# One reduction and one product for a group's counts, and a score leaky that reads PSUM, in a graph attention layer

## The chip, the core and the metric

The kernel runs on one core of a Trainium2 chip. The metric is the time of one execution on the device in microseconds; three runs of the kernel before give a median of 5057.35 us (5054.29 to 5057.92). The core's engines are called PE (matrix products; PEld is its weight load), DVE, ACT, POOL and SP as in the profile. Each runs its own instructions in order, and waits for the others by semaphores. SP only issues DMAs; POOL issues the indirect ones.

## The reference

A graph layer with 12500 nodes of 128 features and 412500 edges of 64 features, with 8 attention heads. The padded tables have 98 blocks of nodes. What matters of it:

```
h, q, k, v = x@Wn+bn, x@Wq+bq, x@Wk+bk, x@Wv+bv;   eh = edges@We + be
hmid   = leaky_relu(concat(q[src], k[tgt], eh) @ A1 + b1, 0.2)
scores = leaky_relu(hmid @ A2 + b2, 0.2)
w      = softmax(scores.mean(-1), over all edges)
out    = segment_sum(w[:, None] * v[tgt], src)
y      = layernorm(h + out) * gamma + beta;   result = layernorm(x + y)
```

The edges come sorted by target. The kernel needs them by source, since the sum runs over sources.

## The kernel before, in words

**Placing.** The edges are cut into 403 groups of 8 tiles of 128 edges, in six parts. For every group the kernel makes a record per edge (edge and target terms of the hidden layer, the value row, the source's lane) and writes the records to a table in DRAM that is ordered by block of source nodes. Where a record goes is counted on the chip: `oh` (L796) is a one-hot of each edge's block out of 99 (98 and a spare one), for 8 tiles as 2 halves of 4. `four` (L806) adds the halves, `few` (L808) adds the remaining four columns to two. PE's `count` (L816) sums `few` over the edges into `pc` in PSUM, one product for each of the two columns, once with the matrix `above` (edges ahead in the tile's lanes) before a group is placed and once with `rest` after it. `ats` (L834) and `pos` (L845) pick each edge's position from `pc`, `idx` (L847) makes it an index. `ohd` (L810) is the one-hot of the targets, by which PE fetches the target rows from `kvs` (L865), adds the edge terms (L871), and ACT copies the result to a record buffer `rec` (L882, L883; six buffers of four tiles). POOL sends each tile of records by an indirect DMA, here called a scatter (L894): 8 for a group, 3224 in all.

**Summing.** A unit is up to two blocks of source nodes with 10, 12 or 14 tiles of records. There are 294 units, 49 in each part. A unit's rows are loaded from the table (`rt`, L1028); its sources' lanes are masked (`sl`, L1050), turned on PE (L1058) into a PSUM tile of the pool `psc`, copied (`slT`, L1065), and spread over the lanes by two DMAs (L1072, L1077). One-hots of them (`ohT`, L1086) fetch the source terms into the hidden layer `ph` (L1097, L1106), whose leaky is a slope copy on ACT (`hm`, L1117) and a max on DVE (L1121). The scores come by L1134 into a PSUM tile of the same pool `psc`, which has **one buffer**: the turn of a later unit and the scores of this one share it. `biased` (L1149, ACT) adds `b2` on the way from PSUM to the SBUF tile `z`. `leaky_scores` (L1157, DVE) takes max(0.2 z, z) in place. `heads` (L1167) adds the heads on PE. Where the tiles of a unit do not divide by four, `biased` and `leaky_scores` have two pieces (96 lanes and 32), and so does each unit of 14 or 10 tiles: 245 units. `maxima`, `reference` and `weights` make the softmax's weights; `select` (`ohs`, L1215), `weigh` (`ohw`, L1229) and `add` (L1258) sum the weighted values.

**Order.** It is written out by hand. Each unit has a list of steps, 8 or 6 per unit. Of a unit that starts at step s with 14 tiles, the scores are at s+9, the bias at s+11, the leaky at s+12, the heads at s+14; the turn of the unit three later is at s+13. A part's units are summed while the next part is placed: a generator `make` yields six times a group, and the steps are dealt out evenly between its yields. What is left after the last group, the last part's 49 units, and the closing (two layer norms) runs without placing.

Of the kernel before, what the change touches and what calls it, by code (L numbers as in the profile page):

```python
# [10 lines left out]
FP = mybir.dt.float32  # L11
BF = mybir.dt.bfloat16
I32 = mybir.dt.int32
U8 = mybir.dt.uint8
AF = mybir.ActivationFunctionType
ALU = mybir.AluOpType
AX = mybir.AxisListType
# [3 lines left out]
P = 128  # L21
# [4 lines left out]
SLOPE = 0.2  # L26
NB = 7
GT = 8
# [334 lines left out]
def first_layer(nc, prep, pprep, WqT, WkT, WeT, Wv, Wn, A1, bq, bk, be, bv, bn, b1):  # L363

    A1s = prep.tile([D, 3, D], FP)
    nc.sync.dma_start(out=A1s, in_=A1.rearrange("(s k) d -> k s d", k=D))
    wT = prep.tile([D, 2, D], FP)
    nc.sync.dma_start(out=wT[:, 0, :], in_=WqT)
    nc.sync.dma_start(out=wT[:, 1, :], in_=WkT)
    weT2 = prep.tile([D, 2, DE], FP)  # L370
    for h in range(2):
        nc.sync.dma_start(out=weT2[:, h, :], in_=WeT)
    cols = prep.tile([D, 3], FP)
    for i, b in enumerate((bq, bk, be)):
        nc.sync.dma_start(out=cols[:, i : i + 1], in_=b)
    W = prep.tile([D, 4, D], FP)
    nc.sync.dma_start(out=W[:, 2, :], in_=Wv)
    nc.sync.dma_start(out=W[:, 3, :], in_=Wn)
    bias = prep.tile([P, 4, D], FP)
    nc.vector.memset(bias[:, 1, :], 0.0)  # L380
    nc.sync.dma_start(out=bias[:, 2, :], in_=bv.to_broadcast([P, D]))
    nc.sync.dma_start(out=bias[:, 3, :], in_=bn.to_broadcast([P, D]))
    b1_b = prep.tile([P, D], FP)
    nc.sync.dma_start(out=b1_b, in_=b1.to_broadcast([P, D]))

    pw = pprep.tile([P, 2, D], FP)
    for s in range(2):
        nc.tensor.matmul(pw[:, s, :], wT[:, s, :], A1s[:, s, :], start=True, stop=True)
    nc.vector.tensor_copy(W[:, 0:2, :], pw)
    pe = pprep.tile([P, D], FP)  # L390
    nc.tensor.matmul(
        pe, weT2.rearrange("k h f -> k (h f)"), A1s[:, 2, :], start=True, stop=True
    )
    WeS = prep.tile([P, D], FP)
    nc.vector.tensor_copy(WeS, pe)

    pb = pprep.tile([P, D], FP)
    for s in range(3):
        nc.tensor.matmul(
            pb, cols[:, s : s + 1].to_broadcast([D, P]), A1s[:, s, :],  # L400
            start=(s == 0), stop=(s == 2),
        )
    nc.vector.tensor_add(bias[:, 0, :], pb, b1_b)
    return W, WeS, bias
# [48 lines left out]
def sorted_path(  # L453
# [8 lines left out]
    nc = tc.nc  # L462
# [3 lines left out]
    NBK = nb + 1  # L466
    EG = GT * P

    const = ctx.enter_context(tc.tile_pool(name="const", bufs=1))
# [24 lines left out]
    nc.vector.memset(A2s, 0.0)  # L494
    nc.scalar.dma_start(out=A2s[:, :H], in_=A2)
    b2_c = const.tile([P, 1], FP)
    nc.vector.memset(b2_c, 0.0)
    headsum = const.tile([P, 4], FP)
    nc.vector.memset(headsum, 0.0)
    for j in range(4):  # L500
        nc.scalar.dma_start(out=b2_c[32 * j : 32 * j + H, :], in_=b2)
        nc.vector.memset(headsum[32 * j : 32 * j + 32, j : j + 1], 1.0)


    fmax = max(
# [12 lines left out]
    def fill(k, n):  # L518

        b, top = 0, plan.tiles[k]  # L520
        while b < nb:
            m = 1
            while m < n and b + m < nb and plan.fill[k][b + m] == plan.fill[k][b]:
                m += 1
            a = plan.cap // P - plan.fill[k][b]
            if a < top:
                yield b, m, a, top - a
            b += m

    def fill_top(k, n):  # L530

        top, most = plan.tiles[k], plan.cap // P
        if top < most:
            for b in range(0, nb, n):
                yield b, min(n, nb - b), top, most - top
# [43 lines left out]
    with tc.tile_pool(name="prep", bufs=1) as prep, tc.tile_pool(  # L579
        name="pprep", bufs=1, space=PSUM  # L580
    ) as pprep, tc.tile_pool(name="pnode", bufs=4, space=PSUM) as pnode:
        W, We_, bias = first_layer(
            nc, prep, pprep, WqT, WkT, WeT, Wv, Wn, A1, bq, bk, be, bv, bn, b1
        )
# [26 lines left out]
    start = const.tile([1, G], I32)  # L611
# [108 lines left out]
    lp = pool("plc", 2)  # L720
# [21 lines left out]
    data, ohds, ohs, few, ats, idxs = {}, {}, {}, {}, {}, {}  # L742
    firsts = []
    pcs = {}
# [15 lines left out]
    def make(p):  # L760


        g0, g1 = plan.parts[p]
# [28 lines left out]
        def onehots(g):  # L792
            if g >= G:
                return
            oh = lp.tile([P, 2, NBK, 4], BF)
            nc.vector.tensor_tensor(  # L796
                oh,
                blk[:, g * GT : (g + 1) * GT]
                .rearrange("p (h o t) -> p h o t", h=2, o=1).to_broadcast([P, 2, NBK, 4]),
                iotaE[:, :NBK, :].rearrange("p (o b) t -> p o b t", o=1)  # L800
                .to_broadcast([P, 2, NBK, 4]),
                op=ALU.is_equal,
            )

            four = one.tile([P, NBK, 4], BF, name="four")
            nc.vector.tensor_add(four, oh[:, 0, :, :], oh[:, 1, :, :])  # L806
            few[g] = lp.tile([P, NBK, 2], BF, name="few")
            nc.vector.tensor_add(few[g], four[:, :, :2], four[:, :, 2:])  # L808
            ohd = wp.tile([P, EG], BF)
            nc.vector.tensor_scalar(ohd, data[g][1], node, None, op0=ALU.is_equal)  # L810
            ohds[g], ohs[g] = ohd, oh


        def count(g, m):
            for i in range(GT // 4):
                nc.tensor.matmul(  # L816
                    pcs[p + (g >= g1)], m, few[g][:, :, i], start=False, stop=False, skip_group_check=True
                )

        def before(g):  # L820
            if g >= G:
                return
            if g == g1:
                ended()
                begin(p + 1)
            elif p == 0 and g == plan.gate:
                gated()
            count(g, above)
# [109 lines left out]
        if p == 0:  # L938
            firsts.append(const.tile([NP, NBK], FP, name="firsts"))
            nc.sync.dma_start(out=firsts[0], in_=bounds[:, 0, :])  # L940
            for g in range(4):
                load(g)
            onehots(0)
            begin(0)
            before(0)
            masked(0)
            places(0)
        for g in range(g0, g1):
            yield
            load(g + 4)  # L950
            if g == g0 + 2:
                limits()
            pk = rows(g, 0)
            after(g)
            onehots(g + 1)
            yield
            evacuate(g, 0, pk)
            yield
            before(g + 1)
            yield  # L960
            pk = rows(g, 2)
            masked(g + 1)
            yield
            evacuate(g, 2, pk)
            idxs.pop(g)
            places(g + 1)
            data.pop(g)
            ohds.pop(g)
            yield
# [19 lines left out]
    state = {}  # L989

    def sums_of(bp):
# [151 lines left out]
        def biased(i):  # L1143
            st = state[i]
            psc, pieces = st["z"]
            z = zp_.tile([P, 4 * P], FP, name="z")
            st["z"] = z, pieces
            for p0, p1, n in pieces:
                nc.scalar.activation(  # L1149
                    z[p0:p1, : n * P], psc[p0:p1, : n * P], AF.Identity, bias=b2_c[p0:p1, :]  # L1150
                )

        def leaky_scores(i):
            z, pieces = state[i]["z"]
            for p0, p1, n in pieces:
                zs = z[p0:p1, : n * P]
                nc.vector.scalar_tensor_tensor(zs, zs, SLOPE, zs, op0=ALU.mult, op1=ALU.max)  # L1157

        def heads(i, t0, m):
            st = state[i]  # L1160
# [124 lines left out]
        for i, (nt, nk, s0, load_at, f, e, turn_at) in enumerate(plans):  # L1285
# [7 lines left out]
            for k in range(nk):  # L1293
                c = 4 * k
                n, s = min(4, nt - c), s0 + 2 * k
# [4 lines left out]
            z = s0 + 2 * nk + 1  # L1300
            do(z, scores, i, 0, nt)
            do(z + 1 + e, biased, i)
            do(z + 2 + e, leaky_scores, i)
            do(z + 3 + 2 * e, heads, i, 0, nt)
            do(f, maxima, i)
# [5 lines left out]
            for j, t0 in enumerate(range(0, nt, 4)):  # L1311
                n = min(4, nt - t0)
# [265 lines left out]
    with tc.manual_schedule():  # L1578
        done = 0
        for p in range(NP + 1):  # L1580
# [8 lines left out]
            if p == 0:  # L1589
                i0 = 0  # L1590
                for k, i1 in enumerate((6 * plan.gate - 12, n0)):
                    pieces = list(fill(k, 2))
# [5 lines left out]
            if 0 < p <= TABS:  # L1598
                pieces = list(fill_top(p - 1, 2))
# [34 lines left out]
def kernel(tc, n, n_edges, x, xT, src, dst, dst_g, bounds, xN, *rest):  # L1634
    nc = tc.nc
    plan = Plan(n, n_edges, x.shape[1], src.shape[1] // GT)
    with tc.tile_pool(name="flag", bufs=1) as fpool:
        flag = fpool.tile([1, 1], I32)
        with ExitStack() as ctx:
            sorted_path(ctx, tc, plan, flag, x, xT, src, dst, dst_g, bounds, xN, *rest)  # L1640
        other = nc.values_load(flag[0:1, 0:1], min_val=0, max_val=1)
        with tc.If(other > 0):
            with ExitStack() as ctx:
                general(ctx, tc, n_edges, x, xT, src, dst, *rest)
# [60 lines left out]
```

## Time and profile before

| | |
|---|---|
| three runs, us | 5054.29, 5057.92, 5057.35 |
| the profiled execution, us | 5054.13 |
| its span, us | 5052.4 |
| mean granted TensorE clock | 0.904 |
| matmuls, DVE and ACT instructions in the page | 32676, 10011, 8487 |
| scatters (L894) | 3224 |

The profile is one execution. A row of groups gives line, engine, operation, tiles written and read with their shapes and count, then busy microseconds and the mean of one in ns, then the engine's idle time just before and who ended it. The rows of waits give engine, waiting line, who ended the wait, microseconds in total, times and the longest. A row of the timeline gives start and duration in microseconds; where it merges several instructions, xN says so and the duration is from the first one's start to the last one's end.

### The profile page before, as it was taken

How to read it: one execution, taken by the hardware profiler on the slowest of the kernel's cores; microseconds unless marked ns; L12 is line 12 of the kernel's file. 1: busy time of each engine (PE TensorE's matmuls, PEld its weight loads, DVE VectorE, ACT ScalarE, POOL GpSimd, SP SyncE). 2: the span in 40 equal slices, each digit the busy share in tenths (PEclk: the TensorE clock that was granted, in tenths of full speed). 3: DMA queues.
4: the chain of work that ended last, by engine and by line, in shares of the span. 5: the costliest groups of instructions: out<-in, count | busy, mean ns of one | idle time of the engine just before them, and what ended most of it. 6: DMA issues, size and time to landing. Idle time of an engine off the chain costs nothing.

```text
span 5052.4 us, 98033 instructions
## 1 busy us (share of the span) xinstructions
PE 4182.9 (83%) x32676; PEld 3101.9 (61%) x32676; DVE 4003.6 (79%) x10011; ACT 3266.3 (65%) x8487; POOL 3352.2 (66%) x3265
## 2 busy tenths in 40 slices
PE   3565568889888888899999899999899999899980
PEld 2343345666666666667776676776677776667760
DVE  6787666778777777789888788888789888777778
ACT  2443345666666666667777677777677777777886
POOL 3777777777777777777777777777777777410002
PEclk6777688999999999999999999999999999999995
DMA  5999789998899998799999899999889999788763
GB/s 187 320 327 358 267 294 330 339 317 290 279 325 328 324 302 288 275 310 324 317 305 309 295 319 310 315 309 312 296 311 327 315 321 313 256 297 285 256 231 140
DMA packets 616502, 1505.48 MB, mean 298 GB/s; under 512 B 104331, under 2 KB 329758, under 8 KB 614193
## 3 DMA queue, kind: packets, MB, share of 16 engines
q1 hardware_dynamic: 461024, 1069.73, 64.9%
q0 software_dynamic: 154752, 429.39, 22.4%
q8 instruction: 259, 4.24, 0.3%
q14 instruction: 259, 2.11, 0.1%
q10 hardware_dynamic: 208, 0.00, 0.0%
HBM read 929.49 MB, written 608.37 MB: 304 GB/s over the span
## 4 chain that ended last, share of the span: by engine, by line
DMA 35%; PE 23%; DVE 17%; POOL 11%; ACT 7%; issue 7%; SPq 1%; ACTq 0%; DVEq 0%; POOLq 0%
DMA rtab<-rec,idx 16%; POOL rtab L894 11%; DMA rt<-rtab 9%; PE psm L1258 5%; DMA row<-slT 4%; PE ph L1106 4%; DMA rowB<-row 3%; PE pkv L871 3%; PE ph L1097 3%; ACT rec L882 2%; PE psc L1134 2%; DVE hm L1121 2%; ACT ohw L1229 2%; PE pkv L865 2%; PE psm L1167 2%
## 5 line engine op out<-in xcount | busy, mean ns | idle before, releaser
L894 POOL DMA_INDIRECT rtab<-rec,idx x3224 | 3291.1, 1021 | 1069.6 <-issue 788.2
L882 ACT ACTIVATE rec<-pkv 128x1024 f32<-128x1024 f32 x806 | 821.0, 1019 | 977.4 <-PE pkv L871 493.9
L1229 ACT ACTIVATE ohw<-ohs,w 128x128 f32<-128x128 bf16 x3822 | 1258.4, 399 | 50.1 <-DVE ohs L1215 40.2
L1258 PE MATMUL psm<-rt,ohw 128*128 128x128 f32 x7644 | 1157.6, 294 | 11.0 <-ACT ohw L1229 11.0
L1258 PEld LDWEIGHTS psm<-rt,ohw 128*128 128x128 f32 x7644 | 997.2, 200 | 59.2 <-ACT ohw L1229 17.7
L1117 ACT ACTIVATE hm<-ph 128x512 f32<-128x512 f32 (+1 forms) x1078 | 582.0, 540 | 430.1 <-PE ph L1106 425.9
L1106 PE MATMUL ph<-ohT,qs 128*128 128x256 bf16 (+3 forms) x4116 | 818.7, 320 | 0.0
L1121 DVE TENSOR_TENSOR hm<-ph,hm 128x512 f32<-128x512 f32 (+1 forms) x1078 | 668.6, 620 | 80.1 <-ACT hm L1117 78.6
L865 PE MATMUL pkv<-kvs,ohd 128*128 128x256 bf16 x3224 | 529.5, 291 | 229.4 <-ACT rec L882 212.1
L1097 PE MATMUL ph<-ident,rt 128*128 128x128 f32 x3822 | 626.3, 282 | 49.3 <-DVE hm L1121 44.9
L871 PE MATMUL pkv<-WeS,eat 64*128 64x128 f32 x6448 | 634.8, 320 | 0.0
L1086 DVE TENSOR_SCALAR ohT<-rowB,iotaP 128x512 bf16<-128x512 uint8 (+1 forms) x1078 | 520.3, 483 | 99.5 <-DMA rowB<-row 94.6
L871 PEld LDWEIGHTS pkv<-WeS,eat 64*128 64x128 f32 x6448 | 468.6, 205 | 190.8 <-issue 186.6
L865 PEld LDWEIGHTS <-ohd 128*128 128x128 bf16 x3224 | 315.4, 103 | 345.7 <-issue 253.5
L1097 PEld LDWEIGHTS ph<-ident,rt 128*128 128x128 f32 x3822 | 469.6, 151 | 68.2 <-DVE hm L1121 53.4
L1106 PEld LDWEIGHTS <-qs 128*128 128x128 bf16 x4116 | 395.5, 100 | 128.5 <-issue 4.8
L1215 DVE TENSOR_TENSOR ohs<-iotaE,sl 128x512 bf16<-128x512 bf16 (+1 forms) x1078 | 430.0, 399 | 48.2 <-ACT ohw L1229 46.6
L834 DVE TENSOR_TENSOR ats<-pc,oh 128x792 f32<-128x792 f32 x403 | 392.1, 973 | 76.9 <-PE pc L816 75.7
L1134 PE MATMUL psc<-hm,A2s 128*32 128x512 f32 (+3 forms) x2352 | 341.5, 545 | 77.9 <-DVE slT L1065 75.0
L845 DVE TENSOR_REDUCE pos<-ats 128x8 f32<-128x792 f32 x403 | 390.3, 969 | 4.2
L1167 PE MATMUL psm<-headsum,z 128*128 128x4 f32 (+1 forms) x2156 | 283.0, 253 | 130.4 <-DVE part L1274 90.4
L1167 PEld LDWEIGHTS psm<-headsum,z 128*128 128x128 f32 (+1 forms) x2156 | 277.2, 200 | 150.1 <-DVE part L1274 105.7
(151 smaller groups left out, 4083.0 us busy)
## 6 DMA issues: line engine op xcount, KB each, us to landing
rt<-rtab SPq DMA_DIRECT2D x196, 1820.0 KB
eat<-in_ea SPq DMA_DIRECT2D x201, 512.0 KB
rt<-rtab SPq DMA_DIRECT2D x49, 1560.0 KB
rt<-rtab SPq DMA_DIRECT2D x49, 1300.0 KB
qs<-qtab SPq DMA_DIRECT2D x294, 192.0 KB
rtab<-rec,idx POOLq DMA_INDIRECT x3224
dstb<-dtab SPq DMA_DIRECT2D x201, 256.0 KB
rtab<-empty SPq DMA_DIRECT2D x98, 520.0 KB
```

The source lines that it names most:

```text
L865: nc.tensor.matmul(pk[:, h, i, :], ohd[:, t * P : (t + 1) * P], kvs, start=(i == 0), stop=False,)
L871: nc.tensor.matmul(pk[:, h, i, :D], eat[h * DE : (h + 1) * DE, (j + i) * P : (j + i + 1) * P], WeS[h * DE : (h + 1) * DE, :], start=False, ...
L882: nc.scalar.activation(rec[:, :, :, : 2 * D], pk, AF.Copy)
L894: one_tile = nc.gpsimd.indirect_dma_start(out=rtab[p % TABS][:, :], out_offset=bass.IndirectOffsetOnAxis(ap=idxs[g][:, t : t + 1], axis=0) ...
L1086: nc.vector.tensor_scalar(st["oh"][k][:, : n * P], st["rowB"][:, t0 * P : (t0 + n) * P], iotaP, None, op0=ALU.is_equal,)
L1097: nc.tensor.matmul(ph[:, j * P : (j + 1) * P], st["rt"][:, t0 + j, :D], ident, is_transpose=True, start=(j == 0), stop=False,)
L1106: nc.tensor.matmul(ph[:, cols], st["qs"][:, j0 // t, s, :], oh[:, cols], start=False, stop=(s == 2 and j1 == t0 + n),)
L1117: nc.scalar.activation(hm, state[i]["ph", k][:, : n * P], AF.Copy, scale=SLOPE)
L1121: nc.vector.tensor_tensor(hm, ph[:, : n * P], hm, op=ALU.max)
L1167: nc.tensor.matmul(st["psS"][:, t0 + j : t0 + j + (nv - 1) * sw + 1 : sw], z[: 32 * nv, j * P : (j + 1) * P], headsum[: 32 * nv, :nv], sta ...
L1229: nc.scalar.activation(ohw[:, j, :], ohs[:, :, j], AF.Copy, scale=st["w"][:, t0 + j : t0 + j + 1])
L1258: nc.tensor.matmul(st["psS"][:, (1 + u) * P : (2 + u) * P], ohw[:, j, :], st["rt"][:, t0 + j, D : 2 * D], start=(k == 0), stop=(k == t - 1),)
```

## The change

The four columns of `four` are summed by one reduction, so `few` has one value per block where it had two, and `count` needs one product where it needed two. In the scores, ACT now writes 0.2 (psc + b2) to `z`, by a scale and a second bias tile `b2_low` made once at the start, and DVE takes the max of (psc + b2) and `z`, so it reads the scores from PSUM a second time, with `b2` added by a per-lane scalar.

```diff
@@ constants
     b2_c = const.tile([P, 1], FP)
+    b2_low = const.tile([P, 1], FP)
...
+    nc.vector.tensor_scalar(b2_low, b2_c, SLOPE, None, op0=ALU.mult)
@@ onehots(g)
             four = one.tile([P, NBK, 4], BF, name="four")
             nc.vector.tensor_add(four, oh[:, 0, :, :], oh[:, 1, :, :])
-            few[g] = lp.tile([P, NBK, 2], BF, name="few")
-            nc.vector.tensor_add(few[g], four[:, :, :2], four[:, :, 2:])
+            few[g] = lp.tile([P, NBK], BF, name="few")
+            with nc.allow_low_precision("counts of up to eight"):
+                nc.vector.tensor_reduce(few[g], four, AX.X, ALU.add)
@@ count(g, m)
-            for i in range(GT // 4):
-                nc.tensor.matmul(
-                    pcs[p + (g >= g1)], m, few[g][:, :, i], start=False, stop=False, skip_group_check=True
-                )
+            nc.tensor.matmul(
+                pcs[p + (g >= g1)], m, few[g], start=False, stop=False, skip_group_check=True
+            )
@@ biased(i)
-            st["z"] = z, pieces
+            st["z"] = z, psc, pieces
             for p0, p1, n in pieces:
                 nc.scalar.activation(
-                    z[p0:p1, : n * P], psc[p0:p1, : n * P], AF.Identity, bias=b2_c[p0:p1, :]
+                    z[p0:p1, : n * P], psc[p0:p1, : n * P], AF.Identity, bias=b2_low[p0:p1, :],
+                    scale=SLOPE,
                 )
@@ leaky_scores(i)
-            z, pieces = state[i]["z"]
+            z, psc, pieces = state[i]["z"]
             for p0, p1, n in pieces:
                 zs = z[p0:p1, : n * P]
-                nc.vector.scalar_tensor_tensor(zs, zs, SLOPE, zs, op0=ALU.mult, op1=ALU.max)
+                nc.vector.scalar_tensor_tensor(
+                    zs, psc[p0:p1, : n * P], b2_c[p0:p1, :], zs, op0=ALU.add, op1=ALU.max
+                )
```

## The prediction

> **What bounds the kernel now.** I read the page's first and fifth parts, then a table of stretches, then POOL's own waits. The stretches show microseconds, then busy time of PE, PEld, DVE, ACT and POOL, then granted clock, DMA share and GB/s.
>
> ```profile
> span 5052.4 us, 98033 instructions
> PE 4182.9 (83%) x32676; PEld 3101.9 (61%) x32676; DVE 4003.6 (79%) x10011; ACT 3266.3 (65%) x8487; POOL 3352.2 (66%) x3265
> L894 POOL DMA_INDIRECT rtab<-rec,idx x3224 | 3291.1, 1021 | 1069.6 <-issue 788.2
> ```
> ```profile
> 0.00:252.00 252.00, 121.92 (x632) 80.41 (x633) 185.38 (x339) 82.41 (x94) 144.24 (x136) 0.72 0.76 253
> 252.00:505.00 253.00, 154.29 (x830) 100.69 (x829) 194.62 (x376) 98.06 (x134) 197.43 (x181) 0.73 1.01 343
> 1010.00:1263.00 253.00, 226.25 (x1860) 168.03 (x1860) 207.14 (x528) 168.50 (x451) 191.71 (x187) 0.94 0.92 304
> 2273.00:2526.00 253.00, 239.60 (x1966) 180.95 (x1966) 221.85 (x544) 189.04 (x502) 194.19 (x194) 0.96 0.92 320
> 4041.00:4294.00 253.00, 236.06 (x1921) 177.21 (x1921) 216.00 (x533) 185.19 (x493) 194.46 (x193) 0.96 0.93 317
> 4547.00:4799.00 252.00, 243.77 (x1873) 186.31 (x1872) 190.60 (x547) 199.74 (x592) 10.44 (x5) 0.99 0.79 270
> ```
> ```profile
> POOL rtab L894 <- issue: 788.2, 2583, 1.2
> POOL rtab L894 <- DMA rtab<-empty: 60.7, 1, 60.7
> POOL rtab L894 <- ACT rec L883: 22.2, 41, 5.8
> ```
>
> Page 1 invites to take PE (83%) or DVE (79%) for the bound. The stretches say otherwise. From 1010 to 4294 us POOL does 187 to 194 scatters in every 253 us, whatever PE and DVE do beside it. A scatter is busy for 1.02 us, and 788.2/2583 = 0.31 us of issue follows each: 1.33 us × 3224 = 4280 us. POOL's idle 1069.6 us is 60.7 of start, 3224 × 0.31 = 983 of issue, and some 25 of true waiting, nearly all of it for records (22.2). So the placing, up to about 4360 us, runs at **POOL's pace**; PE's 95% and DVE's 88% in a middle stretch stand beside it. After 4360 us POOL has nothing to place, PE is busy 243.77 of 252 us, and **PE bounds the tail** of 49 units until the closing.
>
> Two questions decide, then: does the change move POOL's 1.02 us, and does it make PE wait in the tail?
>
> **What lengthens a scatter.** These rows of the timeline (start, duration) give the rule that I use. In the first pair DVE runs a reduce, in the second a max with one input in PSUM, then the score leaky, `oh`, and a chain of `four`, `few` and `ohd`.
>
> ```profile
> 2457.08 0.95 DVE L845 TENSOR_REDUCE pos<-ats 128x8 f32<-128x792 f32 x1
> 2457.89 0.96 POOL L894 DMA_INDIRECT rtab<-rec,idx  x1 [0.30 <-issue]
> 2459.03 0.42 DVE L1121 TENSOR_TENSOR hm<-ph,hm 128x256 f32<-128x256 f32 x1
> 2459.15 0.96 POOL L894 DMA_INDIRECT rtab<-rec,idx  x1 [0.30 <-issue]
> 2464.65 1.12 DVE L1157 SCALAR_TENSOR_TENSOR z<-z 96x512 f32<-96x512 f32 x2 [0.29 <-ACT z L1149]
> 2465.56 1.04 POOL L894 DMA_INDIRECT rtab<-rec,idx  x1 [0.30 <-issue]
> 2470.48 0.56 DVE L796 TENSOR_TENSOR oh<-blk,iotaE 128x792 bf16<-128x792 bf16 x1
> 2470.70 1.17 POOL L894 DMA_INDIRECT rtab<-rec,idx  x1 [0.30 <-issue]
> ...
> 2523.39 0.37 DVE L806 TENSOR_TENSOR four<-oh 128x396 bf16<-128x396 bf16 x1
> 2523.47 1.36 POOL L894 DMA_INDIRECT rtab<-rec,idx  x1 [0.30 <-issue]
> 2523.79 0.26 DVE L808 TENSOR_TENSOR few<-four 128x198 bf16<-128x198 bf16 x1
> 2523.97 0.75 DVE L810 TENSOR_SCALAR ohd<-dstb,node 128x1024 bf16<-128x1024 uint8 x1
> ```
>
> A scatter that starts while the reduce or the PSUM-fed max runs takes 0.96 us. One that starts inside `z` (both inputs in SBUF) ends 0.83 us after it: 2466.60 against 2465.77. One that starts inside `oh` ends at 2471.87, 0.83 after 2471.04. The last one starts inside `four`, and would end 0.83 after it, at 2524.59; it ends at 2524.83, 0.11 after `ohd` (2524.72), so a running `ohd` holds a scatter a second time, about half a microsecond in. So a DVE operation of length d at a scatter's start costs it up to d - 0.13. All of it together is now (1.021 - 0.96) × 3224 = 197 us.
>
> **The change, part by part.**
>
> ```profile
> L808 DVE TENSOR_TENSOR few<-four 128x198 bf16<-128x198 bf16 x403 | 106.3, 264 | 13.7
> L845 DVE TENSOR_REDUCE pos<-ats 128x8 f32<-128x792 f32 x403 | 390.3, 969 | 4.2
> L1196 DVE TENSOR_REDUCE m<-psm 128x1 f32<-128x128 f32 x294 | 82.7, 281 | 6.4 <-PE psm L1188 6.0
> L816 PE MATMUL pc<-few,above 128*128 128x99 bf16 x806 | 107.5, 216 | 132.6 <-DVE few L808 128.3 <-DVE run L919 4.3
> L816 PEld LDWEIGHTS <-above 128*128 128x128 bf16 x806 | 75.6, 102 | 175.2 <-issue 142.7
> L1121 DVE TENSOR_TENSOR hm<-ph,hm 128x512 f32<-128x512 f32 x833 | 567.3, 681 | 48.4 <-ACT hm L1117 47.2
> L1149 ACT ACTIVATE z<-psc,b_c 32x256 f32<-32x256 f32 x196 | 91.6, 467 | 5.0
> L1157 DVE SCALAR_TENSOR_TENSOR z<-z 96x512 f32<-96x512 f32 x196 | 133.6, 681 | 27.8 <-ACT z L1149 27.4
> ```
>
> *The reduce.* It reads 396 elements, and no row shows it. The two reduces bound it by 281 and 969 ns; on the line between them (688 ns over 664 elements) 396 elements take 281 + 268 × 1.036 = 559 ns. I take 559: 295 ns more than `few` has now, 403 times, **119 us more of DVE**, some 7 us in a stretch of 253. DVE's 88% becomes 91% there: hidden behind POOL, unless DVE becomes the pace (a rival).
>
> *The counts.* Four products of a group become two: 806 products and 806 weight loads leave PE. By the weight load (102 ns) that is 82 us, by the matmul's row (216) 174; these rows overlap, so I take 82. It lies wholly in the placing, where POOL sets the pace, and none in the tail. Worth nothing, then, except in the weak stretch below.
>
> *`few` no longer an addition of two SBUF inputs, and `ohd` 0.295 us later.* I spread the scatters' starts evenly over one period of 1.265 us against the chain `oh`, `four`, `few`, `ohd`, and apply the rule. Starting in `oh` (44% of groups): the next scatter starts 0.83 + 0.31 = 1.14 us after `oh` ends. Now some 0.23 us of `ohd` are then left, afterwards 0.52; that is 0.17 to 0.29 us more, 403 × (0.14 × 0.17 + 0.31 × 0.29) = 46 us. Starting in `four` (26%): its hold by `ohd` goes, 0.29 falls to 0.06: 403 × 0.26 × 0.23 = 24 us less. Starting in the gap before `four` (5%) or in `few` and after (24%): 0.2 and 0.08 more, 12 us. Together **+34 us**.
>
> *`z` with PSUM as an input* should stop holding scatters, as the max of L1121 does. Evenly spread, 245 pairs of pieces (0.68 and 0.42 us) cost (0.55² + 0.29²)/(2 × 1.265) = 0.153 us each, 37 us; about a fifth would be caught by the L1086 operation right behind: **-29 us**.
>
> The even spread overshoots, which these two holders show:
>
> ```profile
> L1086 DVE TENSOR_SCALAR ohT<-rowB,iotaP 128x512 bf16<-128x512 uint8 (+1 forms) x1078 | 520.3, 483 | 99.5 <-DMA rowB<-row 94.6
> L1215 DVE TENSOR_TENSOR ohs<-iotaE,sl 128x512 bf16<-128x512 bf16 (+1 forms) x1078 | 430.0, 399 | 48.2 <-ACT ohw L1229 46.6
> ```
>
> By it they cost 1078 × (0.35² + 0.27²)/2.53 = 83 us, `z` 37 and today's chain 0.22 × 403 = 89, in all 209; measured are 197, of which the DMA-filled first two stretches hold about 40 (341.67 us of POOL there against 317 × 0.96), so 157. I scale by 157/209 = three quarters: +25 and -21, **+4 us**. Ends: -40 (the `four` part and all of `z` gained, nothing lost) to +34.
>
> *Lengths of the score leaky.* The L1121 row (681 ns, PSUM) equals L1157's at 512 columns: nothing; ±50 ns on 539 pieces, ±27 us of DVE, would be hidden too. ACT's row stays: a constant scale in place of one. But the first piece on DVE now waits for both ACT pieces in units with two (one semaphore wait instead of two; the order of every engine's instructions is otherwise that of before, minus the counts). At worst 467 ns × 245. The ACT rows above say it hardly bites: in 27.4 us of wait over 196 first pieces DVE is mostly later than ACT anyway. Behind it on DVE stand the next `hm` and `ohT`. I take 0.
>
> *`psc` is held until DVE's leaky has read it* (one buffer, shared with the turn of L1058, one step after the leaky). In the placing PE's wait is covered by the stock of records. In the tail it isn't:
>
> ```profile
> 4504.66 1.12 DVE L1157 SCALAR_TENSOR_TENSOR z<-z 96x512 f32<-96x512 f32 x2
> 4505.31 0.09 PEld L1058 LDWEIGHTS <-sl 128*14 128x14 bf16 x1 [0.42 <-issue]
> ```
>
> The turn would start at 5.78 instead of 5.31, 0.47 us late, and behind it stand PE's products of L1258. Bounds: never, 0; in each of the 49 units by the whole 1.12 us, 55 us. I take a sixth to a quarter of the units, **+4 us**.
>
> *The weak stretch.* Between 860 and 1130 us POOL does wait:
>
> ```profile
> POOL rtab L894 <- ACT rec L883: 11.5, 6, 5.8
> PE pc L816 <- DVE few L808: 9.3, 6, 5.8
> ```
>
> There the records come late and PE waits for `few`. 270/10.6 = 25 groups × (0.295 less 0.1 of PE) = **+5 us**, between 0 and 25 × 0.4 = 10.
>
> *`b2_low`* is one small DVE instruction at the start, while DVE waits for DMAs: 0.
>
> **Sum**: 5054.1 (the profiled execution) + 4 + 5 + 4 = **5067 us**. The profiled execution is 0.06% below the median of 5057.35; I don't add that gap. 5067 is 0.19% above the median, and about 0.2% is what a measurement of this kernel can tell from no change.
>
> **Rivals.**
>
> *POOL is freed* (5023 us). The `z` pieces stop holding scatters, the hold in `four` ends, and the later `ohd` costs nothing because scatters don't start evenly around it: (-29 - 24) × 3/4 = -40, and the small costs (9) stay. For it: reduce and PSUM-fed rows at 0.96. Against: `ohd` at 0.75 us stays the longest holder, and comes to stand alone. [...]
>
> *The moved `ohd` holds more scatters* (5097 us, slower). It ends on the other side of the first rival by one mechanism: 0.295 us between `four` and `ohd` turn one hold of a chain into two. Price +34 unscaled, and `z` gains little because L1086 follows at once: 5054 + 34 + 9. It decides from a mean scatter of 1.03 us on.
>
> *DVE becomes the pace* (5133 us). 119 us more on an engine that already waits in order for ACT, PE and row loads; if two thirds of it shows, 5054 + 79. Against: the records are ready well ahead, as POOL waits only some 25 us for all causes.
>
> *The reduce isn't 559 ns*: at 281 nothing moves and the first rival wins; at 969, 284 us more of DVE, and the third does.
>
> **How the numbers follow.** Forecast, costs nearly cancel (5045 to 5085): 0.50. POOL freed: 0.22. `ohd` in the way: 0.20. DVE the pace: 0.08. Below 5047: 0.22 + 0.03 = 0.25 faster. Of the forecast's 0.50, 0.33 lies within 0.2%, 0.14 above 5067.5: slower 0.14 + 0.20 + 0.08 = 0.42. The range 5020 to 5110 takes in the first two rivals with their spread and leaves out the third and the far ends. The forecast's own range is 5045 to 5085.
>
> **What would show it.** The reduce's row near 559 ns x403; L816 with 806 products; the scatter's mean: 1021 if the holds cancel, about 1009 if POOL is freed, 1031 or more if `ohd` is in the way; scatters that start in `z` at 0.96; the last scatter near 4364 us, later by about 8; L1058 waiting for DVE `z`, and by how much after 4364. If POOL's waits for records grow by tens of microseconds, DVE is the pace and I am wrong; if the scatter's mean stays but the end moves by over 20 us, my picture of the tail is.

## The result, and the profile after

The changed kernel takes 5095.84 us (median of 4 runs, 5086.32 to 5097.28) where the kernel before took 5056.31 in the same session (4 runs, 5054.29 to 5057.92): ratio **1.0073, 95% interval 1.0057 to 1.0089**. That is slower by some 37 us. It lies inside the range (5020 to 5110) but outside the forecast's own 5045 to 5085, 29 us above the forecast, and 1 us from the 5097 of the rival in which the moved `ohd` holds more scatters. The profiled execution took 5096.45 us.

First the page of the changed kernel (span, busy time of the engines, the scatter's group) and POOL's waits:

```profile
span 5094.7 us, 95842 instructions
...
PE 4166.9 (82%) x31427; PEld 3091.8 (61%) x31870; DVE 4168.3 (82%) x10012; ACT 3272.0 (64%) x8487; POOL 3383.6 (66%) x3265
...
L896 POOL DMA_INDIRECT rtab<-rec,idx x3224 | 3321.8, 1030 | 1076.7 <-issue 784.9 <-DMA rtab<-empty 63.1 <-DMA rtab<-rec,idx 56.2
```
```profile
POOL rtab L896 <- issue: 784.9, 2572, 0.8
POOL rtab L896 <- DMA rtab<-empty: 63.1, 2, 62.8
...
POOL rtab L896 <- ACT rec L885: 34.8, 43, 7.4
```

The mean scatter went from 1021 to 1030 ns, and 3321.8 - 3291.1 = 30.7 us of the slowdown are scatters that last longer. Where the rest lies is seen at both ends of the placing. The first two rows are the first and the last scatter of the kernel before, the next two those of the changed one (start, duration):

```profile
63.99 1.23 POOL L894 DMA_INDIRECT rtab<-rec,idx  x1 [60.69 <-DMA rtab<-empty]
4363.05 0.96 POOL L894 DMA_INDIRECT rtab<-rec,idx  x1 [0.30 <-issue]
```
```profile
66.09 1.53 POOL L896 DMA_INDIRECT rtab<-rec,idx  x1 [62.79 <-DMA rtab<-empty]
4400.87 0.96 POOL L896 DMA_INDIRECT rtab<-rec,idx  x1 [0.30 <-issue]
```

The placing ends 37.8 us later: 30.7 of longer scatters, 2.1 of a later start, 5.0 of gaps between scatters. After it the kernel before still had 5052.4 - 4364.0 = 688.4 us to go, the changed one 5094.7 - 4401.8 = 692.9: 4.5 more. Together 42.3 us, the difference of the two spans. The 2.1 and the 5.0 can't be laid to the change: in the first six experiments of the table below the start varies from 63.7 to 65.6 us and the sum of the gaps from 992 to 1006 (1009 before, 1014 after). The stretch behind the placing takes 686 and 688 us in the two kernels with the old scores (counts_only and the kernel before) and 689 to 700 in the six with the new ones, so there the change may cost a few microseconds.

The groups that the change touches, in the changed kernel:

```profile
L811 DVE TENSOR_REDUCE few<-four 128x99 bf16<-128x396 bf16 x403 | 229.1, 568 | 13.7
L813 DVE TENSOR_SCALAR ohd<-dstb,node 128x1024 bf16<-128x1024 uint8 x403 | 311.2, 772 | 4.3 <-DMA dstb<-dtab 3.9 <-PE pkv L867 0.3
L1160 DVE SCALAR_TENSOR_TENSOR z<-psc,b_c,z 96x512 f32<-96x512 f32 x196 | 145.4, 742 | 33.0 <-ACT z L1151 32.7
L1160 DVE SCALAR_TENSOR_TENSOR z<-psc,b_c,z 32x256 f32<-32x256 f32 x196 | 96.7, 493 | 2.8
L818 PE MATMUL pc<-few,rest 128*128 128x99 bf16 x403 | 90.9, 226 | 0.0
L818 PE MATMUL pc<-few,above 128*128 128x99 bf16 x403 | 88.5, 220 | 133.0 <-DVE few L811 125.9 <-DVE run L921 6.7
```

The reduce takes 568 ns against 264 for the old `few`. The first score piece takes 742 ns against 681; the second 493 against 422 in this row of the kernel before:

```profile
L1157 DVE SCALAR_TENSOR_TENSOR z<-z 32x256 f32<-32x256 f32 x196 | 82.7, 422 | 2.8
```

DVE carries 4168.3 - 4003.6 = 165 us more: 123 by `few`, some 35 by the score pieces. PE lost 806 products (403 of each kind are left) and 806 weight loads and is busy for 16 us less; the 16 is rough, since the trace lacks the records of 443 matmuls (31427 against 31870 weight loads). In the stretches (columns as in the prediction) DVE has risen to 226 of 253 us while POOL's scatters go on at 192 to 193 a stretch:

```profile
2273.00:2526.00 253.00, 235.93 (x1854) 177.68 (x1887) 226.07 (x534) 186.99 (x492) 194.26 (x193) 0.95 0.92 313
4041.00:4294.00 253.00, 232.93 (x1843) 176.10 (x1874) 226.38 (x535) 186.47 (x496) 194.73 (x192) 0.96 0.92 314
```

**One group, before and after.** DVE's and POOL's rows of the timeline, from one `oh` to the end of its `ohd`; first the kernel before, then the changed one. In both a scatter starts 0.33 to 0.35 us into `oh`.

```profile
2299.31 0.56 DVE L796 TENSOR_TENSOR oh<-blk,iotaE 128x792 bf16<-128x792 bf16 x1
2299.66 1.05 POOL L894 DMA_INDIRECT rtab<-rec,idx  x1 [0.30 <-issue]
2299.91 0.37 DVE L806 TENSOR_TENSOR four<-oh 128x396 bf16<-128x396 bf16 x1
2300.31 0.26 DVE L808 TENSOR_TENSOR few<-four 128x198 bf16<-128x198 bf16 x1
2300.49 0.75 DVE L810 TENSOR_SCALAR ohd<-dstb,node 128x1024 bf16<-128x1024 uint8 x1
2301.01 1.06 POOL L894 DMA_INDIRECT rtab<-rec,idx  x1 [0.30 <-ACT w L1206]
```
```profile
2301.33 0.56 DVE L798 TENSOR_TENSOR oh<-blk,iotaE 128x792 bf16<-128x792 bf16 x1
2301.66 1.06 POOL L896 DMA_INDIRECT rtab<-rec,idx  x1 [0.30 <-DMA rtab<-rec,idx]
2301.92 0.37 DVE L808 TENSOR_TENSOR four<-oh 128x396 bf16<-128x396 bf16 x1
2302.32 0.57 DVE L811 TENSOR_REDUCE few<-four 128x99 bf16<-128x396 bf16 x1
2302.81 0.74 DVE L813 TENSOR_SCALAR ohd<-dstb,node 128x1024 bf16<-128x1024 uint8 x1
2303.03 1.37 POOL L896 DMA_INDIRECT rtab<-rec,idx  x1 [0.30 <-issue]
```

The first scatter is held by `oh` in both, and its successor therefore starts 1.70 us after `oh` began, in both. Before, `ohd` has 0.23 us left by then, and the second scatter lasts 1.06. After, `ohd` began 0.30 us later and has 0.52 left; the scatter lasts 1.37. In both kernels the second scatter ends 0.83 to 0.85 us after `ohd` does: it is held, for 0.10 us before and for 0.41 after.

Counted over all rows from 600 us on (where POOL is past the crowded start): time of scatters beyond 0.96 us, by the DVE operation that runs at the scatter's start (the one that began last, where two overlap).

| runs at the start | before: scatters, mean ns over, sum us | after |
|---|---|---|
| `oh` | 154, 152, 23.4 | 174, 155, 27.0 |
| `four` | 113, 209, 23.6 | 104, 49, 5.1 |
| `few` | 43, 50, 2.1 | 70, 212, 14.9 |
| `ohd` | 201, 86, 17.2 | 288, 266, **76.6** |
| `z` | 160, 165, 26.4 | 190, 0, **0.0** |
| `ohT` | 259, 95, 24.5 | 238, 67, 16.0 |
| `ohs` | 135, 133, 18.0 | 140, 137, 19.2 |
| all | 2849, 50, 143.0 | 2860, 57, 163.0 |

That is 20.0 of the 30.7 us. The other 10.7 fall before 600 us, and there it is the same chain: scatters that start in `ohd` run over by 2.2 us in all before and 9.4 after, those in `few` by 0.3 and 3.7.

### The profile page after: what moved, and what is told of

Its sections match the earlier page's. It is cut to its first block, busy times and chain, and to the rows that moved or that the text cites. A ratio compares the mean times of both kernels' runs of the same rounds, so it can differ in the third digit from the quotient of the medians.

```text
span 5094.7 us, 95842 instructions
## 1 busy us (share of the span) xinstructions
PE 4166.9 (82%) x31427; PEld 3091.8 (61%) x31870; DVE 4168.3 (82%) x10012; ACT 3272.0 (64%) x8487; POOL 3383.6 (66%) x3265
## 4 chain that ended last, share of the span: by engine, by line
DMA 33%; PE 23%; DVE 20%; POOL 10%; issue 7%; ACT 6%; SPq 1%; DVEq 0%; ACTq 0%; POOLq 0%
DMA rtab<-rec,idx 14%; POOL rtab L896 10%; DMA rt<-rtab 10%; PE psm L1263 6%; PE ph L1108 4%; DMA row<-slT 3%; DVE hm L1123 3%; PE pkv L873 3%; PE ph L1099 3%; PE psc L1136 2%; DMA rowB<-row 2%; PE pkv L867 2%; ACT rec L884 2%; PE psm L1172 2%; DVE z L1160 2%
## 5 line engine op out<-in xcount | busy, mean ns | idle before, releaser
L896 POOL DMA_INDIRECT rtab<-rec,idx x3224 | 3321.8, 1030 | 1076.7 <-issue 784.9
L1263 PE MATMUL psm<-rt,ohw 128*128 128x128 f32 x7644 | 1169.5, 297 | 3.5 <-ACT ohw L1234 3.4
L1263 PEld LDWEIGHTS psm<-rt,ohw 128*128 128x128 f32 x7644 | 1009.8, 202 | 87.5 <-issue 23.3
L1108 PE MATMUL ph<-ohT,qs 128*128 128x512 bf16 (+3 forms) x3673 | 725.2, 314 | 25.6 <-issue 3.2
L1088 DVE TENSOR_SCALAR ohT<-rowB,iotaP 128x512 bf16<-128x512 uint8 (+1 forms) x1078 | 509.5, 473 | 82.7 <-DMA rowB<-row 74.6
```

What stands on the lines that cost most here:

```text
L896: one_tile = nc.gpsimd.indirect_dma_start(out=rtab[p % TABS][:, :], out_offset=bass.IndirectOffsetOnAxis(ap=idxs[g][:, t : t + 1], axis=0) ...
L1088: nc.vector.tensor_scalar(st["oh"][k][:, : n * P], st["rowB"][:, t0 * P : (t0 + n) * P], iotaP, None, op0=ALU.is_equal,)
L1108: nc.tensor.matmul(ph[:, cols], st["qs"][:, j0 // t, s, :], oh[:, cols], start=False, stop=(s == 2 and j1 == t0 + n),)
L1263: nc.tensor.matmul(st["psS"][:, (1 + u) * P : (2 + u) * P], ohw[:, j, :], st["rt"][:, t0 + j, D : 2 * D], start=(k == 0), stop=(k == t - 1),)
```

## The experiments

The theory: scatters last longer because `ohd` comes 0.3 us later in the chain, and the placing pays for it one to one. Rivals: DVE, 165 us busier, sets the pace (1); the scores part costs, by its longer `z` and by `psc` being held (2); `few` or `ohd` comes late for PE and the records (3). Eight kernels ran where the kernel before took 5046 to 5053 us. In the table the ratios are of medians, each to the kernel before of its own session; the sums are of one profiled execution each, against that of the kernel before (3291.1 and 4003.6 us):

| kernel | scatter mean ns; sum over before, us | DVE busy over before, us | ratio (95%) |
|---|---|---|---|
| the change | 1030; +30.7 | +165 | 1.0073 (1.0057 to 1.0089) |
| counts_only | 1039; +57.4 | +129 | 1.0108 (1.0094 to 1.0123) |
| scores_only | 1016; -14.0 | +45 | 0.9974 (0.9964 to 0.9984) |
| reduce_behind_ohd | 1041; +63.9 | +116 | 1.0133 (1.0118 to 1.0148) |
| reduce_of_eight | 1024; +10.7 | +155 | 1.0026 (1.0017 to 1.0035) |
| idle_reduce | 1036; +48.8 | +341 | 1.0094 (1.0079 to 1.0110) |
| zero_products | 1033; +38.4 | +163 | 1.0057 (1.0044 to 1.0071) |
| ohd_from_psum | 1002; -60.7 | +341 | 1.0142 (1.0127 to 1.0158) |
| scores_and_ohd_from_psum | 1002; -59.9 | +228 | 1.0065 (1.0048 to 1.0082) |

In the first seven rows the time follows the sum of the scatters within 0.2%. With 0.1% of the time as 5 us, +63.9 us would be 1.0126, +57.4 1.0114, +48.8 1.0097, +38.4 1.0076, +30.7 1.0061, +10.7 1.0021, -14.0 0.9972; the worst is zero_products, 1.0076 for a measured 1.0057. DVE's busy time orders nothing: the kernel with 116 us more is slower than the one with 341. The last two rows have another wait, which is told below.

### counts_only

Against the kernel before:

```
-            few[g] = lp.tile([P, NBK, 2], BF, name="few")
-            nc.vector.tensor_add(few[g], four[:, :, :2], four[:, :, 2:])
+            few[g] = lp.tile([P, NBK], BF, name="few")
+            with nc.allow_low_precision("counts of up to eight"):
+                nc.vector.tensor_reduce(few[g], four, AX.X, ALU.add)
...
-            for i in range(GT // 4):
-                nc.tensor.matmul(
-                    pcs[p + (g >= g1)], m, few[g][:, :, i], start=False, stop=False, skip_group_check=True
-                )
+            nc.tensor.matmul(
+                pcs[p + (g >= g1)], m, few[g], start=False, stop=False, skip_group_check=True
+            )
```

> Only the counts part: the reduce and one product a pass; the scores as in the kernel before. Theory (the moved ohd holds scatters): ohd stands as late as in the changed kernel and the z pieces hold scatters again, which cost some 25 us more there; scatter mean 1037 to 1040 ns, time 5110 to 5125 us, slower than the whole change. Rival 1 (DVE sets the pace): DVE carries 123 of the change's 165 us, so three quarters of the 40 us: about 5086 us, and the scatter mean is no guide. Rival 2 (the cost comes with the scores part: longer z, psc held): about 5056 us.

The group of its scatters:

```profile
L894 POOL DMA_INDIRECT rtab<-rec,idx x3224 | 3348.5, 1039 | 1062.8 <-issue 789.1 <-DMA rtab<-empty 61.0 <-DMA rtab<-rec,idx 52.9
```

5100.17 us against 5045.62, a ratio of 1.0108; by the base of 5056 that is 5111. The scatter's mean and the time are the theory's, and the counts part alone is slower than the whole change, which rival 1 excludes. Rival 2 is out. The sum of the scatters is 26.7 us above that of the whole change, which is what `z` holds in the kernel before (26.4 from 600 us on; 25.0 here).

### scores_only

Against the kernel before, the main lines:

```
-            st["z"] = z, pieces
+            st["z"] = z, psc, pieces
...
-                nc.vector.scalar_tensor_tensor(zs, zs, SLOPE, zs, op0=ALU.mult, op1=ALU.max)
+                nc.vector.scalar_tensor_tensor(
+                    zs, psc[p0:p1, : n * P], b2_c[p0:p1, :], zs, op0=ALU.add, op1=ALU.max
+                )
```

> Only the scores part; the counts as in the kernel before. Theory: z no longer holds scatters and ohd stays where it was, scatter mean about 1012 ns, time 5025 to 5040 us. Rival 1 (DVE sets the pace): 35 to 40 us more of DVE in z, about 5065 us. Rival 2 (the scores part costs): about 5095 us.

```profile
L896 POOL DMA_INDIRECT rtab<-rec,idx x3224 | 3277.1, 1016 | 1067.2 <-issue 784.1 <-DMA rtab<-empty 62.3 <-DMA rtab<-rec,idx 50.1
```

5033.28 us against 5045.62: faster by 0.26%, with 45 us more of DVE. The sign is the theory's, the size is smaller: by the ratio 13 us where 16 to 31 were expected, and 1016 ns where 1012 was. From 600 us on the scatters run over by 124.7 us in place of 143.0, so 18 of the 26 us of `z` remain. This part alone beats both kernels.

### reduce_behind_ohd

Against the changed kernel, as the edits below unless the text says otherwise:

```
+            ohd = wp.tile([P, EG], BF)
+            nc.vector.tensor_scalar(ohd, data[g][1], node, None, op0=ALU.is_equal)
             few[g] = lp.tile([P, NBK], BF, name="few")
             with nc.allow_low_precision("counts of up to eight"):
                 nc.vector.tensor_reduce(few[g], four, AX.X, ALU.add)
-            ohd = wp.tile([P, EG], BF)
-            nc.vector.tensor_scalar(ohd, data[g][1], node, None, op0=ALU.is_equal)
```

> The changed kernel with the reduce issued behind ohd in place of ahead of it: the same instructions and the same DVE work, ohd 0.5 us earlier. Theory: the second hold of a chain by ohd goes; replaying POOL by the hold rule over the changed kernel's DVE rows in this order gives 30 to 55 us less of held time, scatter mean about 1014 ns, time 5040 to 5065 us. Rival 1 (DVE sets the pace): 5096 us as before the swap, since DVE is as busy. Rival 3 (few late for PE): later than 5096 us, as few comes 0.75 us later.

It went the other way: 5111.07 us, ratio 1.0133, mean 1041, where 5040 to 5065 us and 1014 ns were expected. One group of its timeline:

```profile
2266.53 0.56 DVE L798 TENSOR_TENSOR oh<-blk,iotaE 128x792 bf16<-128x792 bf16 x1
2266.80 1.47 POOL L896 DMA_INDIRECT rtab<-rec,idx  x1 [0.30 <-ACT ohw L1234]
2267.12 0.37 DVE L808 TENSOR_TENSOR four<-oh 128x396 bf16<-128x396 bf16 x1
2267.40 0.75 DVE L810 TENSOR_SCALAR ohd<-dstb,node 128x1024 bf16<-128x1024 uint8 x1
2268.07 0.56 DVE L813 TENSOR_REDUCE few<-four 128x99 bf16<-128x396 bf16 x1
```

The scatter started in `oh`, should have ended 0.83 after it (2267.92), and ended at 2268.27, 0.12 after `ohd`. So do nearly all: 98% of the 158 scatters that start in `oh` are held, by 483 ns in the mean against 155 in the changed kernel. It is as if a scatter asked a second time, 0.48 us after its start, or, if it was held, some 0.35 us after the holder's end. (In the changed kernel the scatters that no operation held at their start, and behind which `ohd` began, were held in all 58 cases where `ohd` began 0.25 to 0.45 us after them and in none of 5 from 0.50 us on; the 0.35 is 0.83 - 0.48.) Here `ohd` runs from 0.31 to 1.06 us after `oh`'s end and is met; in the kernel before it starts 0.62 after, in the changed one 0.92 after. My expectation had the rule but put 0.03 us between all operations; the rows show that `ohd` starts 0.09 us before the end of `four`, whose result it doesn't read (behind `few` it is 82 ns in the median in the kernel before and 86 in the changed one), and that tenth of a microsecond moved `ohd` from just behind the asking to across it. With the spacing of the rows the same rule gives more held time for this order than for the changed kernel's (measured from 600 us on: 194.2 against 163.0 us). That was worked out afterwards, so this run doesn't count as a forecast that came true. Rival 1 is refuted either way (no more DVE work, 0.6% slower). Rival 3 had forecast a later time too, but POOL waits 23.7 us for `rec` here, less than the 34.8 of the changed kernel.

### reduce_of_eight

```
-            four = one.tile([P, NBK, 4], BF, name="four")
-            nc.vector.tensor_add(four, oh[:, 0, :, :], oh[:, 1, :, :])
+            ohd = wp.tile([P, EG], BF)
+            nc.vector.tensor_scalar(ohd, data[g][1], node, None, op0=ALU.is_equal)
             few[g] = lp.tile([P, NBK], BF, name="few")
             with nc.allow_low_precision("counts of up to eight"):
-                nc.vector.tensor_reduce(few[g], four, AX.X, ALU.add)
-            ohd = wp.tile([P, EG], BF)
-            nc.vector.tensor_scalar(ohd, data[g][1], node, None, op0=ALU.is_equal)
+                nc.vector.tensor_reduce(few[g], oh.rearrange("p h b t -> p b h t"), AX.XY, ALU.add)
```

> The changed kernel without four: the order is oh, ohd, and one reduce of all eight columns (792 elements in, as long as pos, 0.97 us). Theory: one holder fewer, ohd directly behind oh so that one hold covers both; scatter mean 1010 to 1015 ns, time 5035 to 5060 us. Rival 1 (DVE sets the pace): DVE work is nearly that of the changed kernel (0.97 against 0.37 + 0.57 us), 5096 us. Rival 3 (few late for PE): above 5096 us.

```profile
L894 POOL DMA_INDIRECT rtab<-rec,idx x3224 | 3301.8, 1024 | 1061.8 <-issue 781.7 <-DMA rtab<-empty 62.4 <-DMA rtab<-rec,idx 56.4
```

5059.62 us against 5045.62, ratio 1.0026: with nearly the DVE work of the change (+155 against +165 us) it loses a third of what the change loses. The mean is 1024, above the expected 1010 to 1015; the direction is the theory's, the size isn't.

### ohd_from_psum and scores_and_ohd_from_psum

```
+    bank = pcp.tile([P, 4 * P], FP, name="pc")
+    node_ps = bank[:, 4 * P - 1 :]
+    nc.vector.tensor_copy(node_ps, node)
...
-        pcs[p] = pcp.tile([P, NBK], FP, name="pc")
+        pcs[p] = bank[:, :NBK]
...
-            nc.vector.tensor_scalar(ohd, data[g][1], node, None, op0=ALU.is_equal)
+            nc.vector.tensor_tensor(
+                ohd, data[g][1], node_ps.to_broadcast([P, EG]), op=ALU.is_equal,
+            )
```

The first kernel has this edit on the changed one, the second on scores_only.

> The changed kernel, where ohd compares with node kept in one column of PSUM (an is_equal of two tensors, one of them in PSUM) in place of the one-input compare; its place among DVE's instructions stays. ats (792 elements, one input in PSUM) takes 974 ns, so 1024 elements some 1.25 us, 0.5 us more than now, 200 us more of DVE. Theory (ohd holds scatters): no scatter is held by ohd any more; POOL replayed by the hold rule over the changed kernel's rows without that holder has 78 to 90 us less of held time; scatter mean 1004 to 1007 ns, time about 5015 us. Rival (DVE sets the pace): with 200 us more, at three quarters, about 5240 us.

> The same ohd from PSUM with the scores part alone (the counts as in the kernel before). Theory: replay without ohd as a holder gives 86 us of held time after 600 us against 125 measured in scores_only, 40 us less: scatter mean about 1004 ns, time about 4995 us. Rival (DVE sets the pace): 200 us more of DVE, about 5180 us.

Two groups and one of POOL's waits in ohd_from_psum:

```profile
L901 POOL DMA_INDIRECT rtab<-rec,idx x3224 | 3230.4, 1002 | 1196.8 <-issue 758.5 <-ACT rec L890 134.0 <-DMA eat<-in_ea 62.6
...
L816 DVE TENSOR_TENSOR ohd<-dstb,pc 128x1024 bf16<-128x1024 uint8 x403 | 489.6, 1215 | 210.3 <-PE pc L823 205.0 <-DMA dstb<-dtab 3.3 <-DMA qs<-qtab 1.5
```
```profile
POOL rtab L901 <- ACT rec L890: 134.0, 115, 6.9
```

The first half came out as forecast, or nearly: none of the 303 scatters that start with over 0.2 us of `ohd` left is held, the mean falls to 1002, and the held time after 600 us falls by 75.9 us to 87.1, where the replay gave 78 to 90 less (83.7 for 86 in the other kernel). But the time rose, to 1.0142 and 1.0065, where 5015 and 4995 us were expected. `node` now lies in the tile of the counts, and `ohd` waits 205 us for PE's products into it (270 in the other kernel); behind it DVE's work is late, and POOL waits 134 us for records (140). So it is shown that `ohd` makes scatters longer; what their shortening is worth is hidden here by a wait of my making.

### idle_reduce and zero_products

The first line stands behind `ohd`, the second behind each count, with a tile of zeros.

```
+            nc.vector.tensor_reduce(idle, four, AX.X, ALU.add)
```
```
+            nc.tensor.matmul(pcs[...], m, none[:, :NBK], ...)
```

> The changed kernel with a second reduce of four behind ohd, whose result nobody reads: 0.57 us more of DVE a group, 229 us in all, with no holder moved against another inside the chain. Theory: the placing stays at POOL's pace, 5085 to 5115 us, scatter mean 1025 to 1038 ns. Rival (DVE sets the pace; the change's 165 us of DVE cost 40): 5095 + 229 x 40/165 = 5150 us or more.

> The changed kernel with a second product in each count, by a tile of zeros, so that PE has as many count products and weight loads as before the change. Theory: PE's relief was worth nothing while POOL paces the placing: within 10 us of the changed kernel, 5085 to 5105 us. Rival (PE's share is worth something and was spent by the holds): 20 to 80 us more, 5115 us or later.

idle_reduce, the engines' busy time, its scatters, and the added group:

```profile
PE 4160.0 (82%) x31427; PEld 3075.2 (60%) x31870; DVE 4344.3 (85%) x10415; ACT 3275.2 (64%) x8487; POOL 3401.2 (67%) x3265
...
L899 POOL DMA_INDIRECT rtab<-rec,idx x3224 | 3339.9, 1036 | 1066.3 <-issue 776.2 <-DMA rtab<-empty 60.4 <-DMA rtab<-rec,idx 49.5
```
```profile
L816 DVE TENSOR_REDUCE idle<-four 128x99 bf16<-128x396 bf16 x403 | 224.4, 557 | 0.0
```

It carries 176 us more of DVE than the changed kernel and takes 5103.46 us, ratio 1.0094 (1.0079 to 1.0110): not the 5150 that rival 1 asks for. Its interval overlaps that of the change, and its 18 us of longer scatters would cover the difference. zero_products gives PE its products back and runs 5083.38 us, ratio 1.0057 (1.0044 to 1.0071), just below the expected 5085 to 5105; its interval overlaps that of the change too. PE's relief was worth nothing that can be seen.

### ohd behind ats: not to be read

Four runs issued `ohd` behind `ats`, which has waited for the counts anyway: psum_ohd_behind_ats (the change), scores_psum_ohd_behind_ats and its repeat (the scores part), scores_ohd_behind_ats (the scores part, `ohd` in its old form).

```
-            nc.vector.tensor_scalar(ohd, data[g][1], node, None, op0=ALU.is_equal)
...
+            nc.vector.tensor_tensor(
+                ohds[g], data[g][1], node_ps.to_broadcast([P, EG]), op=ALU.is_equal,
+            )
```

> ohd_from_psum with ohd issued behind ats of the same group, which has waited for the count's products already; otherwise the changed kernel. Theory: no scatter is held by ohd, and the wait of ohd for pc that ate the gain in ohd_from_psum (205 us of it; POOL's waits for rec 134 us) goes: scatter mean 1002 to 1006 ns, time 5010 to 5030 us. Rival (DVE sets the pace; DVE is as busy as in ohd_from_psum): it stays near 5129 us.

> The same with the scores part alone (the counts as in the kernel before). Theory: scatter mean 1002 to 1006 ns, time 4990 to 5015 us, faster than either kernel. Rival (DVE sets the pace): near 5092 us, as scores_and_ohd_from_psum.

> scores_only with ohd (its one-input form, unchanged) issued behind ats in place of behind few: the same instructions, the chain of holders split in two. Theory (a late ohd holds scatters of its own): replay of scores_only's rows gives 35 us more of held time after 600 us, scatter mean about 1027 ns, time about 5070 us. Rival (DVE sets the pace): the same DVE work, 5033 us. Rival 3 (a later ohd starves PE and the records): POOL's wait for rec grows from 23 us to 100 us or more.

> The kernel of scores_psum_ohd_behind_ats once more, since there the kernel before took 6175 us as well and POOL waited 960 us for records, so that nothing could be read about a placing paced by POOL. Where the kernel before takes 5040 to 5060 us: theory, scatter mean 1002 to 1006 ns, POOL's wait for rec back to some 25 to 40 us from the 140 of scores_and_ohd_from_psum, time 4990 to 5015 us. Rival (DVE sets the pace: it carries some 240 us more than in the kernel before): near 5092 us, as scores_and_ohd_from_psum, with the wait for rec still above 100 us.

They fell on two chips on which the kernel before takes 6165 to 6175 us too. The scatters of the repeat and its wait, and `ohd` in it:

```profile
L901 POOL DMA_INDIRECT rtab<-rec,idx x3224 | 3200.5, 993 | 2349.3 <-ACT rec L890 979.4 <-issue 844.2 <-ACT by L1258 100.7
```
```profile
L844 DVE TENSOR_TENSOR ohd<-dstb,pc 128x1024 bf16<-128x1024 uint8 x403 | 487.6, 1210 | 2.1 <-DMA dstb<-dtab 2.1
```

POOL waits 979 us for records there (833 to 961 in the other three): the placing isn't at POOL's pace, and shorter scatters can't show in the time (ratios 1.0118, 1.0150, 1.0126 and, in the old form, 1.0040). Two things can be read: `ohd` no longer waits for the counts (2.1 us in place of 270), and scatters held by `ohd` in its PSUM form stay away (mean 991 to 994 ns). In the old form the mean was 1012 ns where 1027 was expected. Whether that kernel beats scores_only where POOL sets the pace stays open, and so does the split chain in the old form.

## Why the prediction came out as it did

- **What bounds the kernel: right.** The change and six other kernels follow the sum of their scatters, and neither 176 us more of DVE nor 806 more products moves them by more.
- **The reduce: right.** 559 ns forecast, 568 measured; 119 us more of DVE, 123 measured; hidden, as idle_reduce shows.
- **The counts at nothing: right**, as far as zero_products can tell.
- **`ohd` 0.295 us later, "together +34 us", scaled to +25: this step failed, by its size.** Summed over a group's chain (all scatters that start between the start of `oh` and the end of `ohd`, 352 groups from 600 us on) the scatters run over by 196 ns a group before, 350 after (352 in counts_only). That is +154 ns, 54 us over these groups and 62 over 403: 28 us above the +34, and 37 above the +25 that went into the sum. The shares that I spread were fair: before, the first scatter of 44% of the chains starts in `oh` (forecast 44), of 32% in `four` (26), of 8% between two operations (5), of 16% in `few` or `ohd` (24). The prices weren't. Starting in `oh` costs 247 ns before and 528 after: +0.28, the upper end of the 0.17 to 0.29 that I had. Starting in `four` loses its 209 ns at the first scatter (now 49), but the chain as a whole only falls from 224 to 157: the freed successor starts earlier and meets `ohd`, so -0.07 and not -0.23. Starting in `few` rises from 50 to 225: the scatter isn't held by the reduce, but is held later by `ohd`; I had +0.08 for most of these.
- **Scaling by three quarters: wrong, with little effect.** It mended an overshoot of the old sum by pulling the new loss down with it. The overshoot lay mostly elsewhere: `ohT` and `ohs` hold 42.5 us from 600 us on where the even spread gave 83, the old chain 79 us (196 ns × 403) where it gave 89. In the sum it moved 1 us only, since gain and loss shrank alike (+5 unscaled, +4 scaled). Behind a hold there is no even spread: a scatter held by `oh` or `z` starts its successor 1.13 to 1.14 us behind the holder's end, and what stands at that distance is met again and again.
- **`z` stops holding: right.** 26.4 us to 0.0 (from 600 us on), where -29 stood, scaled -21. Of the scatters that start in it from 600 us on, 80% of 160 were held before and 1% of 190 after.
- **`z` as long as before: wrong, without effect.** 61 to 71 ns more a piece, some 35 us of DVE. scores_only carries them and is faster. The `hm` row that I went by (681 ns with one input in PSUM) doesn't show it, and why the pieces last longer no run shows.
- **`psc` held: right.** The changed kernel's waits after 4404 us have this row, 6.8 us and 14 of the 49 units where I took 4 us and 8 to 12; the kernel before has no such row after 4364 us:

```profile
PE psc L1060 <- DVE z L1160: 6.8, 14, 1.1
```

- **The weak stretch: +5 forecast.** POOL's wait for `rec` between 860 and 1130 us goes from 11.5 to 15.4 us. That is no more than what this wait differs by between the kernels above (22.2 to 34.8 us over the whole run), so the +5 isn't shown. The tail's 4.5 us fit the +4 for `psc`, but the six tails with the new scores differ by 11 us among themselves.

So the forecast that costs nearly cancel failed, by the price of the later `ohd`. The second rival gave 5097 and 5096 was measured, by its mechanism and at its own point of decision (1030 ns). Its numbers were wrong on both sides, though: the chain cost 62 us and not 34, and `z` gained in full, which it denied. That the two met within 1 us is luck. The rival of a freed POOL is refuted as a whole; its scores half is right. That DVE becomes the pace is refuted.

## What to carry to other kernels

Where POOL's DMAs set the pace, as here, an operation on DVE can cost by where it falls against them more than by its length (idle_reduce added 176 us of DVE for some 10 us): look up which operations a scatter waits for, and how far behind one holder the next one starts. Taking a holder out of a chain can cost time if the others move apart. The gain of one half of a change (the scores, 0.9974) can be lost to the other (the counts, 1.0108); try the halves alone. A sum that overshoots a measured total isn't mended by one factor on all its terms.

## What the runs showed of the hardware

- A scatter lasts 0.96 us in the median, in the kernel before and in the changed one, and here it was held in two places. The first is its start. Of the scatters from 600 us on that started 0.1 us or more into a DVE operation and had 0.2 us or more of it left, these ended 0.83 us after it (before, after): `oh` 71 of 71, 97 of 97; `ohs` 55 of 60, 58 of 63; `ohT` 136 of 137, 72 of 72; `ohd` 137 of 138, 188 of 190; `z` 81 of 81 before, none of 108 after, where it reads PSUM; `four` 21 of 21 after, while the 23 before met `ohd` as well and ended 1.08 us after `four`. The reduce `pos` held none of 178 and none of 185. Of all 174 that start in `oh` in the changed kernel, 72% were held.
- The second place is some 0.48 us in. Of the scatters that started in none of these holders, in both kernels from 600 us on, all 84 over which `ohd` began 0.09 to 0.45 us after their start ended 0.12 us after it, and so did 16 of the 17 over which an `ohT` of 512 columns began up to 0.45 us after their start and ended more than 0.86 us after it. `oh` held none of the 59 over which it ran at 0.48 us and past 0.86.
- The same compare as an operation of two inputs, the second in PSUM, takes 1215 ns in place of 772 and holds none of 303 scatters (ohd_from_psum).
- With a constant in a corner of the PSUM tile that PE counts into, its reader waited for those matmuls: 205 to 270 us over 403 groups. Whether the chip asks for that wait or only the program's semaphores do, no run shows.
- On two chips the kernel before took 6165 to 6175 us, at a mean granted TensorE clock of 0.83 to 0.84 where it is 0.90 to 0.91 elsewhere. The edited kernels profiled there waited up to 979 us for records on POOL while the DVE operations kept their lengths (`ohd` from PSUM 1210 ns against 1215). Many of the waits there (496 us of ACT's for `hm` in the repeat) are put down to no engine of this core; the cause stays open.
